# Six key blocks to a batch, and norms, reciprocals and layouts that keep channels on partitions

## The chip, the core and the metric

The kernel runs on one core of one Trainium2 chip. The metric is the device time of one execution in microseconds (us). Five engines work side by side, each on its own queue of instructions in program order: PE (TensorE, matrix products into PSUM), DVE (VectorE), ACT (ScalarE), POOL (GpSimd) and SP (SyncE, which issues DMAs here). They wait for each other by semaphores.

## What is computed

A block of depthwise convolution and attention over four images of 384 channels and 48 x 48 pixels (2304 tokens), in float32:

```python
x_flat = x.reshape(B, C, N).transpose(0, 2, 1)
local = lax.conv_general_dilated(x, conv_w, ..., feature_group_count=C)   # 7 x 7, one filter per channel
local = local * inv[None, :, None, None] + (bn_beta - bn_mean * inv)[None, :, None, None]
x_norm = _layernorm(x_flat, ln_gamma, ln_beta)
q, k, v = split(x_norm @ qkv_w.T + qkv_b)                # 8 heads of 48
q = q + heads(_layernorm(local_flat, ln_gamma, ln_beta))
attn = jax.nn.softmax(jnp.einsum('bhnd,bhmd->bhnm', q, k) * scale, axis=-1)
out = jnp.einsum('bhnm,bhmd->bhnd', attn, v)
out = x_flat + out @ proj_w.T + proj_b
```

## The kernel before

Channels lie on 128 partitions, in three chunks. A **tile** is one image's group of 384 tokens (8 pixel rows): 6 groups of 4 images make 24 tiles. For each tile the queries of the eight heads are held as four pairs (two heads of 48 rows, at partitions 0 and 64). For each pair, `attention` runs over the 18 blocks of 128 keys: two score products (L455) into a PSUM tile `s`, one exponential on ACT (L463, 128 x 768) into `pt`, and two products with the values (L431) that accumulate into `o`; a column of ones beside the values gives the sum of the exponentials. Blocks are taken two to a batch (`BATCH`): the scores of a batch are issued, then the value products of the batch before.

The rest is put beside that as generators in a deque, `behind`, of which a few steps are taken per batch: `q_part` (the 147 convolution taps of the next tile on DVE, L266 and L270, then the layer norms and the query projection L207), `kv_part` (keys and values of the next image, L207 and L229), `pair_output` and `group_output` (division and output projection L379). Norms want the tokens on partitions: `normalized` transposes each 128 x 128 block on PE (L153), takes mean and variance on DVE (L157, L158), the inverse root on POOL (L161), normalizes on DVE (L165), and `x_normalized` transposes back (L191). The convolution's norm is transposed back at L288, the attention output before its division at L343 (after copies out of PSUM on ACT and DVE, L439 and L440) and after it at L369.

A scheduler in the tile framework sets the final order of each engine's queue from the order in which the code is written and from its own estimate of when things are ready. The engines then keep that order on the chip.

A branch after the pass repeats the work with shifted exponents if a sum of exponentials was out of range (`inside`); in the profile shown here it is not taken.

Of the kernel before, what the change touches and what calls it, by code (L numbers as in the profile page):

```python
# [14 lines left out]
P = 128  # L15
NH = 8
# [4 lines left out]
BATCH = 2  # L21
RG = 8
SAFE = 1e15
AHEAD = 1
# [5 lines left out]

@with_exitstack
def attention_pass(
# [13 lines left out]
    shifted: bool,  # L48
    inside=None,
# [14 lines left out]
    HS = HA if shifted else HD  # L64
# [3 lines left out]
    kv = ctx.enter_context(tc.tile_pool(name="kv", bufs=NG + AHEAD))  # L68
    ps_s = ctx.enter_context(tc.tile_pool(name="ps_s", bufs=2, space=bass.MemoryType.PSUM))
    ps_o = ctx.enter_context(tc.tile_pool(name="ps_o", bufs=2, space=bass.MemoryType.PSUM))  # L70
    ps_m = ctx.enter_context(tc.tile_pool(name="ps_m", bufs=2, space=bass.MemoryType.PSUM))
# [263 lines left out]
    def pair_output(b, g, p, osb):  # L335

        if p == 0:
            outputs[b, g] = work.tile([P, NB, NH, HD], F32, tag="ao", name="ao", bufs=1)
        ao = outputs[b, g]
        tp = psum()  # L340
        ot = tp[:, :G].rearrange("p (t h d) -> p t h d", t=NB, h=2)
        for blk in range(NB):
            nc.tensor.transpose(  # L343
                tp[:, blk * P : blk * P + KP],
                osb[0:KP, blk * P : (blk + 1) * P],
                ident[0:KP, 0:KP],
            )
        rden = work.tile([P, NB, 2, 1], F32, tag="rden", name="rden")
        nc.vector.reciprocal(rden, ot[:, :, :, HD:HA])
        if inside is not None:  # L350

            flat = rden.rearrange("p t h o -> p (t h o)")
            for bound, op in ((SAFE, ALU.is_le), (1 / SAFE, ALU.is_ge)):
                nc.vector.scalar_tensor_tensor(inside, flat, bound, inside, op, ALU.mult)
# [57 lines left out]
    weighing = []  # L412
    divisions = deque()

    def weigh_last():
        if weighing:
            weighing.pop()()

    def attention(b, g, p, ahead, units):


        q = queries[b, g][p]
        o = ps_o.tile([P, 512], F32, tag="o", name="o")
        osb = work.tile([P, G], F32, tag="osb", name="osb")
        nc.gpsimd.memset(osb[32:64, :], 0.0)  # L425

        def weigh(batch):
            for kb, pt in batch:
                for j in range(2):
                    r = 64 * j  # L430
                    nc.tensor.matmul(  # L431
                        o[r : r + HA, :G],
                        lhsT=values[b, kb // NB][:, kb % NB, 2 * p + j, :],
                        rhs=pt[:, j, :],
                        start=kb == 0,
                        stop=kb == KB - 1,
                    )
            if batch[-1][0] == KB - 1:
                nc.scalar.copy(osb[0:HA, :], o[0:HA, :G])  # L439
                nc.vector.tensor_copy(osb[64 : 64 + HA, :], o[64 : 64 + HA, :G])  # L440
                divisions.append((b, g, p, osb))

        for k0 in range(0, KB, BATCH):
            while divisions:
                done = divisions.popleft()
                if done[2] == NP - 1:
                    behind.appendleft(group_output(*done[:2]))
                behind.appendleft(pair_output(*done))
            batch = []
            for kb in range(k0, k0 + BATCH):  # L450
                s = ps_s.tile([P, 2, 512], F32, tag="s", name="s")
                blk = kb % NB
                for j in range(2):
                    r = 64 * j
                    nc.tensor.matmul(  # L455
                        s[:, j, :G],
                        lhsT=keys[b, kb // NB][r : r + HS, p, blk * P : (blk + 1) * P],
                        rhs=q[r : r + HS, :],
                        start=True,
                        stop=True,  # L460
                    )
                pt = work.tile([P, 2, G], F32, tag="pt", name="pt", bufs=2 * BATCH)
                nc.scalar.activation(pt, s[:, :, :G], AF.Exp, scale=SCALE)  # L463
                batch.append((kb, pt))
            weigh_last()
            weighing.append(lambda batch=batch: weigh(batch))
            for _ in range(BATCH):
                if ahead is not None:
                    next(ahead, None)
            advance(BATCH * units)  # L470
        if ahead is not None:
            for _ in ahead:
                pass

# [4 lines left out]
    for b in range(B):  # L479
        if shifted:  # L480
            for _ in max_part(b, 0, 0):
                pass
        for g in range(NG):
            for p in range(NP):
                ahead = None
                if p == (NP - 1 if shifted else 0):
                    finish()
                if shifted and p < NP - 1:
                    ahead = max_part(b, g, p + 1)
                elif shifted and g < NG - 1:  # L490
                    ahead = max_part(b, g + 1, 0)
                if p == 0:
                    if g < NG - 1:
                        behind.append(q_part(b, g + 1))
                    elif b < B - 1:
                        for ga in range(AHEAD):
# [4 lines left out]
                attention(b, g, p, ahead, 5 if shifted else 3)  # L501
        weigh_last()
        while divisions:
            behind.append(pair_output(*divisions.popleft()))
        behind.append(group_output(b, NG - 1))
        if b < B - 1:
            for ga in range(AHEAD, NG):
                behind.append(kv_part(b + 1, ga))
        finish()


def conv_attention(tc: tile.TileContext, *args):
    nc = tc.nc
    with tc.tile_pool(name="keep", bufs=1) as keep:
        inside = keep.tile([P, 6], F32, tag="inside", name="inside")
        outside = keep.tile([P, 6], F32, tag="outside", name="outside")
        ones = keep.tile([P, 1], F32, tag="ones_col", name="ones_col")
        total = keep.tile([1, 1], F32, tag="total", name="total")
        flag = keep.tile([1, 1], mybir.dt.int32, tag="flag", name="flag")
        nc.vector.memset(inside, 1.0)  # L520
        nc.vector.memset(ones, 1.0)
        attention_pass(tc, *args, shifted=False, inside=inside)
        nc.vector.tensor_scalar(outside, inside, 0.5, None, ALU.is_lt)
        with tc.tile_pool(name="ps_f", bufs=1, space=bass.MemoryType.PSUM) as ps_f:
            count = ps_f.tile([1, 6], F32, tag="count", name="count")
            nc.tensor.matmul(count, lhsT=ones, rhs=outside, start=True, stop=True)
            nc.vector.tensor_reduce(total, count, AX.X, ALU.add)
        nc.vector.tensor_copy(flag, total)
        n_outside = nc.values_load(flag[0:1, 0:1])
        with tc.If(n_outside > 0):  # L530
            attention_pass(tc, *args, shifted=True)
# [51 lines left out]
```

## Time and profile before

| | us |
|---|---|
| median of 3 runs (lowest, highest) | 4068.94 (4068.04, 4070.35) |
| profiled execution | 4069.32 |
| its span | 4067.5 |
| PE busy in it | 3792.6 (93%) |
| DVE busy | 2347.7 (58%) |
| ACT busy | 1695.6 (42%) |
| mean granted TensorE clock | 0.947 of full |

A matmul of float32 operands shows as two records in the profile, so the 3456 calls of L455 are 6912 records. Matmul ends are modelled, so a busy PE is not a PE at its peak: start-to-start distances tell more than durations. A releaser in brackets names what ended an engine's idle time.

### The profile page before, as it was taken

How to read it: one execution, taken by the hardware profiler on the slowest of the kernel's cores; microseconds unless marked ns; L12 is line 12 of the kernel's file. 1: busy time of each engine (PE TensorE's matmuls, PEld its weight loads, DVE VectorE, ACT ScalarE, POOL GpSimd, SP SyncE). 2: the span in 40 equal slices, each digit the busy share in tenths (PEclk: the TensorE clock that was granted, in tenths of full speed). 3: DMA queues.
4: the chain of work that ended last, by engine and by line, in shares of the span. 5: the costliest groups of instructions: out<-in, count | busy, mean ns of one | idle time of the engine just before them, and what ended most of it. 6: DMA issues, size and time to landing. Idle time of an engine off the chain costs nothing.

```text
span 4067.5 us, 45598 instructions
## 1 busy us (share of the span) xinstructions
PE 3792.6 (93%) x17714; PEld 1655.5 (41%) x17714; DVE 2347.7 (58%) x4908; ACT 1695.6 (42%) x2449; POOL 189.5 (5%) x325
## 2 busy tenths in 40 slices
PE   5889999999999999999999998999999999999999
PEld 3434433344454343334445333433344433333443
DVE  7577647647553584674564548548548364764610
ACT  1244343453434434445433443443443344344444
POOL 1000000000000000000000000000000000000000
PEclk9889899999999999999999999999999999999999
DMA  2000000000000000000000000000000000000000
GB/s 61 1 1 7 5 3 6 3 39 6 7 0 1 7 6 1 7 6 36 7 6 1 1 7 7 1 7 6 36 7 6 1 1 7 7 3 5 7 7 7
DMA packets 20419, 33.97 MB, mean 8 GB/s; under 512 B 8416, under 2 KB 18656, under 8 KB 18656
## 3 DMA queue, kind: packets, MB, share of 16 engines
q1 hardware_dynamic: 12096, 28.32, 1.8%
q10 hardware_dynamic: 8096, 2.65, 0.3%
q8 instruction: 140, 2.29, 0.2%
q14 instruction: 87, 0.71, 0.1%
HBM read 16.80 MB, written 14.16 MB: 8 GB/s over the span
## 4 chain that ended last, share of the span: by engine, by line
PE 61%; DVE 34%; POOL 2%; issue 1%; ACT 1%; DMA 0%; ACTq 0%; POOLq 0%; DVEq 0%
DVE acc L270 27%; PE s L455 24%; PE o L431 20%; PE pm L207 7%; PE pm L379 3%; PE pm L229 2%; DVE st L157 2%; PE pm L191 2%; POOL rs L161 1%; DVE xt L165 1%; PE pm L153 1%; DVE q L293 1%; PE pm L343 1%; PE pm L369 1%; DVE osb L440 1%
## 5 line engine op out<-in xcount | busy, mean ns | idle before, releaser
L270 DVE SCALAR_TENSOR_TENSOR acc<-x,cw,acc 128x368 f32<-128x368 f32 (+10 forms) x3456 | 1872.1, 589 | 35.4
L463 ACT ACTIVATE pt<-s 128x768 f32<-128x768 f32 x1728 | 1316.1, 808 | 1307.2 <-PE s L455 1306.8
L455 PE MATMUL s<-q,k 48*128 48x384 f32 x6912 | 1551.1, 526 | 1.2 <-ACT pt L463 1.2
L431 PE MATMUL o<-pt,v 128*49 128x384 f32 x6912 | 1330.6, 505 | 0.0
L455 PEld LDWEIGHTS s<-q,k 48*128 48x128 f32 x6912 | 648.8, 190 | 697.3 <-ACT pt L463 364.7
L431 PEld LDWEIGHTS o<-pt,v 128*49 128x49 f32 x6912 | 381.8, 125 | 825.5 <-issue 823.3
L440 DVE COPY osb<-o 49x384 f32<-49x384 f32 x96 | 53.8, 560 | 759.5 <-ACT osb L439 757.8
L207 PE MATMUL pm<-xnT,w_qk 128*128 128x384 f32 x1152 | 424.8, 517 | 0.3 <-ACT q L214 0.3
L157 DVE BATCH_NORM_STATS2 st<-xt 128x6 f32<-128x384 f32 x216 | 113.4, 551 | 409.8 <-ACT xt L154 408.8
L207 PEld LDWEIGHTS pm<-xnT,w_qk 128*128 128x128 f32 x1152 | 219.7, 200 | 183.3 <-issue 24.8
L191 PE MATMUL pm<-ident,xt 128*128 128x128 f32 x432 | 103.4, 354 | 107.2 <-DVE xt L165 99.9
L194 ACT ACTIVATE xnT<-pm,ln_sb 128x384 f32<-128x384 f32 x144 | 92.4, 669 | 238.6 <-PE pm L191 238.6
L154 ACT COPY xt<-pm 128x384 f32<-128x384 f32 x216 | 98.2, 481 | 217.2 <-PE pm L153 183.1
L379 PE MATMUL pm<-aoT,w_o 128*128 128x384 f32 x432 | 182.1, 578 | 0.0
L343 PE MATMUL pm<-ident,osb 113*128 113x113 f32 x288 | 51.1, 288 | 105.9 <-DVE osb L440 105.9
L214 ACT ACTIVATE q<-pm,qkb 128x384 f32<-128x384 f32 x96 | 55.8, 581 | 224.7 <-PE pm L207 224.7
L229 PE MATMUL pm<-w_v,xnT 128*128 128x384 f32 x432 | 144.0, 487 | 5.4 <-DVE v L236 5.4
L191 PEld LDWEIGHTS pm<-ident,xt 128*128 128x128 f32 x432 | 60.5, 168 | 194.2 <-issue 75.7
L236 DVE TENSOR_TENSOR v<-pm,vb 128x384 f32<-128x384 f32 x72 | 39.9, 555 | 154.4 <-PE pm L229 154.3
L379 PEld LDWEIGHTS pm<-aoT,w_o 128*128 128x128 f32 x432 | 96.7, 234 | 75.4 <-issue 31.6
L425 POOL MEMSET osb<- 32x384 f32 x96 | 39.9, 416 | 1802.1 <-PE pm L343 1648.7
L214 ACT ACTIVATE k<-pm,qkb 128x384 f32<-128x384 f32 x96 | 55.8, 581 | 147.3 <-PE pm L207 147.3
(52 smaller groups left out, 1047.7 us busy)
## 6 DMA issues: line engine op xcount, KB each, us to landing
x<-in_x_dram SPq DMA_DIRECT2D x12, 1152.0 KB, 7.5
out_dram<-xr SPq DMA_DIRECT2D x72, 192.0 KB, 1.8
w_qk<-in_qkv_wT_dram ACTq DMA_DIRECT2D x6, 192.0 KB, 5.0
w_v<-in_qkv_wT_dram ACTq DMA_DIRECT2D x3, 192.0 KB, 5.6
w_o<-in_proj_wT_dram ACTq DMA_DIRECT2D x3, 192.0 KB, 3.7
vb<-in_v_b_dram ACTq DMA_DIRECT2D x1, 192.0 KB, 4.5
cw<-in_conv_w_dram ACTq DMA_DIRECT2D x1, 73.5 KB, 5.8
ln_p<-in_ln_pair_dram ACTq DMA_DIRECT2D x2, 1.5 KB, 4.5
```

The costliest lines, as they stand in the source:

```text
L154: nc.scalar.copy(xt[:, blk, :], tp[:, :C])
L157: nc.vector.bn_stats(st[:, blk, :], xt[:, blk, :])
L191: nc.tensor.transpose(tp[:, blk * P : (blk + 1) * P], kept["xn"][:, blk, c * P : (c + 1) * P], ident)
L207: nc.tensor.matmul(ps[:, :G], lhsT=w_qk[:, c, which, 2 * p : 2 * p + 2, :].rearrange("p h d -> p (h d)"), rhs=xnT[:, c, :], start=c == 0, ...
L214: nc.scalar.activation(dst, ps[:, :G], AF.Identity, bias=qkb[:, which, p : p + 1])
L229: nc.tensor.matmul(ps[:, :C], lhsT=xnT[:, c, blk * P : (blk + 1) * P], rhs=w_v[:, c, :], start=c == 0, stop=c == CC - 1,)
L270: nc.vector.scalar_tensor_tensor(dst, src, cw[:, c, t : t + 1], dst, ALU.mult, ALU.add)
L379: nc.tensor.matmul(ps[:, :G], lhsT=w_o[:, c, co * P : (co + 1) * P], rhs=aoT[:, c, :], start=c == 0, stop=c == CC - 1,)
L431: nc.tensor.matmul(o[r : r + HA, :G], lhsT=values[b, kb // NB][:, kb % NB, 2 * p + j, :], rhs=pt[:, j, :], start=kb == 0, stop=kb == KB - 1,)
L440: nc.vector.tensor_copy(osb[64 : 64 + HA, :], o[64 : 64 + HA, :G])
L455: nc.tensor.matmul(s[:, j, :G], lhsT=keys[b, kb // NB][r : r + HS, p, blk * P : (blk + 1) * P], rhs=q[r : r + HS, :], start=True, stop=True,)
L463: nc.scalar.activation(pt, s[:, :, :G], AF.Exp, scale=SCALE)
```

## The change

The pass that runs is written anew as `unshifted_pass`; the old function remains as `shifted_pass` behind the branch. What is different in the new one:

- **Layout.** Weights and activations are loaded so that rows 0 to 47 and 64 to 111 of the three chunks hold heads 0 to 5, and rows 48 to 63 and 112 to 127 hold a third each of heads 6 and 7 (`segments`). Queries and keys come from 3 instead of 4 projections; six small DMAs (`gather_tails`) collect the last two heads into one more tile, and six give them back after attention.
- **Norms.** Sums over chunks on DVE (`chunk_sum`), a matmul with a matrix of 1/384 that leaves the mean on every partition (`spread_mean`), subtraction on DVE and square on ACT (`centre`), the same again for the variance, the inverse root by Ln and Exp on ACT (`inverse_root`) with one Newton step on DVE. No PE transposes are left. Gain and offset go into the weights once.
- **Division.** The sums go to DRAM as one row per head (`den`), come back as 128 x 24, one reciprocal is taken, it goes to DRAM again (`rden`) and comes back spread over partitions (`rb`); one product divides the tile (`divide`, one per tile).
- **Batches.** Six key blocks to a batch, so three batches to a pair and 12 **slots** to a tile. PSUM: three score tiles of two banks (`ring`), one bank for the outputs (`sums`), one for all else (`bank`). `pt` has nine buffers.
- **Convolution.** From slabs of the image (`load_slab`), two accumulators `acc`, the taps spread over slots (`convolve`). Keys and values of the next image are made between images (`keys_values`), all six groups in a row; its x is normalized during the image before.

```diff
-BATCH = 2
+BATCH = 6
+NSLOT = 12
+X_SLOT, OUT_SLOT, LN_SLOT = 3, 5, 9
...
+    def chunk_sum(src):
+        s = work.tile([P, G], F32, tag="sum", name="sum")
+        nc.vector.tensor_add(s, src[:, 0, :], src[:, 1, :])
+        nc.vector.tensor_add(s, s, src[:, 2, :])
+        return s
...
+        nc.tensor.matmul(m[:, :G], lhsT=mean_w, rhs=s, start=True, stop=True)
...
+    def centre(src, m):
+        nc.vector.tensor_sub(src, src, over_chunks(m[:, :G]))
+        sq = work.tile([P, CC, G], F32, tag="sq", name="sq", bufs=1)
+        nc.scalar.activation(sq, src, AF.Square)
+        return sq
...
+        nc.scalar.activation(u, m[:, :G], AF.Ln, bias=eps)
+        nc.scalar.activation(y, u, AF.Exp, scale=-0.5)
+        nc.scalar.activation(u, y, AF.Square)
...
+    def newton(m, y, u):
+        nc.vector.scalar_tensor_tensor(u, m[:, :G], eps, u, ALU.add, ALU.mult)
+        nc.vector.scalar_tensor_tensor(u, u, -1.0, y, ALU.add, ALU.mult)
+        nc.vector.scalar_tensor_tensor(y, u, -0.5, y, ALU.mult, ALU.add)
...
+    def query_end(t, rs):
...
+        nc.vector.tensor_mul(acc, acc, over_chunks(rs))
+        for c in range(CC):
+            nc.vector.scalar_tensor_tensor(
+                q[:, c, :], acc[:, c, :], gain[:, c : c + 1], q[:, c, :], ALU.mult, ALU.add
+            )
+        gather_tails(q3, q)
...
+    def divide(t):
...
+        nc.sync.dma_start(out=rd, in_=den.rearrange(flat, f=few))
+        nc.vector.reciprocal(rd, rd)
+        nc.sync.dma_start(out=rden.rearrange(flat, f=few), in_=rd)
...
+    for t in range(NT):
+        b, g = divmod(t, NG)
+        if g == 0 and b:
+            weigh()
+            for gk in range(NG):
+                convolve(("kv", t, gk), 0)
+                keys_values(b, gk)
+                convolve(("kv", t, gk), 1)
...
+        for s in range(NSLOT):
+            point = ("slot", t, s)
+            scores(t, s)
+            convolve(point, 0)
...
+            if s < CC and following:
+                query_step(t + 1, s)
+            if s == X_SLOT and coming:
+                held["m"] = spread_mean(held.pop("s"))
+                held["sq"] = centre(xn[b + 1, g], held.pop("m"))
+            if s == X_SLOT + 1 and coming:
+                m = spread_mean(held.pop("s"))
+                held["root"] = m, *inverse_root(m)
+            if s in range(OUT_SLOT, OUT_SLOT + CC) and t:
+                output_step(t - 1, s - OUT_SLOT)
+            if s == LN_SLOT and following:
+                held["m"] = spread_mean(held.pop("s"))
+                held["sq"] = centre(accs[t + 1], held.pop("m"))
+            if s == LN_SLOT + 1 and following:
+                m = spread_mean(held.pop("s"))
+                held["root"] = m, *inverse_root(m)
+            if weighing[0][0] != t or s:
+                weigh()
+            convolve(point, 1)
...
+            if s == LN_SLOT + 1 and following:
+                query_end(t + 1, newton(*held.pop("root")))
```

What the scheduler makes of it shows in the queues. **PE in the middle of a pair**, before: a row is a run of products, `s` are scores, `o` the value products, `k_2` and `v_2` the key and value group 2.

```order
L455 MATMUL s<-q_1_2_1631,k_2_357 128x384 x2
L455 MATMUL s<-q_1_2_1631,k_3_441 128x384 x2
L431 MATMUL o<-pt,v_2_358 49x384 x4
L455 MATMUL s<-q_1_2_1631,k_3_441 128x384 x4
L431 MATMUL o<-pt,v_2_358 49x384 x2
L431 MATMUL o<-pt,v_3_442 49x384 x2
```

The same place now; `r` is a score tile, `m` the query projection of the next tile, and line 446 stands for 455, line 459 for 431.

```order
L446 MATMUL r<-q_844,k_2_474 128x384 x6
L446 MATMUL r<-q_844,k_3_557 128x384 x6
L268 MATMUL m<-xn_2_124,w_qk 128x384 x3
L459 MATMUL o<-pt,v_0_293 49x384 x6
L459 MATMUL o<-pt,v_1_393 49x384 x6
```

Four scores alternated with four value products; now twelve alternate with twelve, with one other step between at most.

**DVE at a result that PE waits for**, before: taps (L270, `acc`), and among them the copy of a finished pair's output (L440), without which PE cannot transpose it at L343.

```order
L266 TENSOR_SCALAR acc_934<-x0_83,cw_94,shift_134 128x384
L270 SCALAR_TENSOR_TENSOR acc_934<-x0_83,cw_94,acc_934 128x8x47
L270 SCALAR_TENSOR_TENSOR acc_934<-x0_83,cw_94,acc_934 128x8x45
L270 SCALAR_TENSOR_TENSOR acc_934<-x0_83,cw_94,acc_934 128x8x46
L440 COPY osb_920<-o_919 49x384
```

DVE now, in slot 3 of the second tile: the subtraction of the mean from the next image's x (L245), more taps (L203), and the sums of squares (L234, L235 of `sq`) that PE needs for its matmul in slot 4.

```order
L245 TENSOR_TENSOR xn1_1_1610<-xn1_1_1610,m_1820 128x1152
L203 SCALAR_TENSOR_TENSOR acc3_2196<-slab0_3_1401,cw_182,acc3_2196 128x384
L203 SCALAR_TENSOR_TENSOR acc3_2196<-slab0_3_1401,cw_182,acc3_2196 128x8x47
L203 SCALAR_TENSOR_TENSOR acc3_2196<-slab0_3_1401,cw_182,acc3_2196 128x8x46
L203 SCALAR_TENSOR_TENSOR acc3_2196<-slab0_3_1401,cw_182,acc3_2196 128x8x45 x2
L234 TENSOR_TENSOR sum_1850<-sq_1823 128x384
L234 TENSOR_TENSOR sum_2158<-acc2_1406 128x384
L235 TENSOR_TENSOR sum_1850<-sum_1850,sq_1823 128x384
```

Between the end of the previous norm (`query_end`) and the first row of this piece stand 109 taps, one reciprocal and the division; the sums stand behind 114 taps. All taps here are those of `acc3`, one tile ahead of the norm that they stand in front of.

## Rows read from the trace of the kernel before

**Rows 1.** Costliest groups: line, operation, count, busy us, mean ns, idle before.

```profile
L270 DVE SCALAR_TENSOR_TENSOR acc<-x,cw,acc 128x368 f32<-128x368 f32 (+10 forms) x3456 | 1872.1, 589 | 35.4
L463 ACT ACTIVATE pt<-s 128x768 f32<-128x768 f32 x1728 | 1316.1, 808 | 1307.2 <-PE s L455 1306.8
L455 PE MATMUL s<-q,k 48*128 48x384 f32 x6912 | 1551.1, 526 | 1.2 <-ACT pt L463 1.2
```

**Rows 2.** PE's waits: who for whom, us in total, times, longest.

```profile
PE pm L343 <- DVE osb L440: 105.9, 34, 8.1
```

**Rows 3.** Order of time, DVE, 193 to 240 us: start, length, what, count.

```profile
193.02 35.07 DVE L270 SCALAR_TENSOR_TENSOR acc<-x,cw,acc 128x360 f32<-128x360 f32 x68
...
230.05 0.56 DVE L440 COPY osb<-o 49x384 f32<-49x384 f32 x1
...
234.37 0.20 DVE L349 RECIPROCAL rden<-pm 128x6 f32<-128x6 f32 x1
```

**Rows 4.** Order of time, PE, 212 to 238 us, with idle time before and its releaser.

```profile
230.67 0.83 PE L343 MATMUL pm<-ident,osb 113*128 113x113 f32 x3 [8.13 <-DVE osb L440]
231.43 2.93 PE L455 MATMUL s<-q,k 48*128 48x384 f32 x8
...
236.91 1.56 PE L455 MATMUL s<-q,k 48*128 48x384 f32 x8
```

**Rows 5.** Stretches: us, busy of PE, PEld, DVE, ACT, POOL, PEclk, DMA, GB/s.

```profile
231.00:237.00 6.00, 6.00 (x21) 2.09 (x19) 5.75 (x14) 1.62 (x2) 0.41 (x1) 0.52 0.01 3
237.00:258.00 21.00, 21.00 (x116) 8.26 (x118) 19.83 (x34) 11.06 (x15) 0.00 (x0) 1.00 0.00 1
```

**Rows 6.** Order of time, PE, 500 to 515 us.

```profile
505.36 0.92 PE L455 MATMUL s<-q,k 48*128 48x384 f32 x4
506.21 1.50 PE L431 MATMUL o<-pt,v 128*49 128x384 f32 x8
507.64 2.20 PE L379 MATMUL pm<-aoT,w_o 128*128 128x384 f32 x6
509.77 1.56 PE L455 MATMUL s<-q,k 48*128 48x384 f32 x8
511.26 1.50 PE L431 MATMUL o<-pt,v 128*49 128x384 f32 x8
512.69 1.56 PE L455 MATMUL s<-q,k 48*128 48x384 f32 x8
```

**Rows 7.** Order of time, all engines, exponentials at 510 us.

```profile
510.79 1.51 ACT L463 ACTIVATE pt<-s 128x768 f32<-128x768 f32 x2 [3.60 <-PE s L455]
```

**Rows 8.** Order of time, PE, key and value projections at 1145 us.

```profile
1144.79 7.91 PE L207 MATMUL pm<-xnT,w_qk 128*128 128x384 f32 x24
1152.54 5.97 PE L229 MATMUL pm<-w_v,xnT 128*128 128x384 f32 x18
```

**Rows 9.** Groups by form, the small operations that price new ones.

```profile
L165 DVE TENSOR_SCALAR xt<-xt,mv,rs 128x384 f32<-128x384 f32 x144 | 61.6, 483 | 55.4 <-POOL rs L161 55.4
...
L439 ACT COPY osb<-o 49x384 f32<-49x384 f32 x96 | 45.4, 473 | 60.1 <-PE o L431 56.3 <-issue 3.8
L386 DVE SCALAR_TENSOR_TENSOR xr<-pm,pb,xr 128x384 f32<-128x384 f32 x72 | 44.3, 615 | 43.7 <-PE pm L379 43.4
```

**Rows 10.** Order of time, the first taps, and the first score products.

```profile
15.95 8.69 DVE L270 SCALAR_TENSOR_TENSOR acc<-x,cw,acc 128x225 f32<-128x225 f32 x18
...
185.49 0.91 PE L455 MATMUL s<-q,k 48*128 48x384 f32 x2
```

**Rows 11.** DMA issues: what, count, KB each, median us from issue to landing.

```profile
out_dram<-xr SPq DMA_DIRECT2D x72, 192.0 KB, 1.8
...
cw<-in_conv_w_dram ACTq DMA_DIRECT2D x1, 73.5 KB, 5.8
```

**Rows 12.** Order of time, the last 15 us.

```profile
4054.09 7.13 PE L379 MATMUL pm<-aoT,w_o 128*128 128x384 f32 x18
...
4061.25 0.62 DVE L386 SCALAR_TENSOR_TENSOR xr<-pm,pb,xr 128x384 f32<-128x384 f32 x1 [1.32 <-PE pm L379]
```

More of the change, by code (lines that the diff above doesn't have):

```diff
@@ new lines, in conv_attention @@
+def conv_attention(tc: tile.TileContext, *args):
+    nc = tc.nc
+    few = NH * RG * 48 // P
+    with tc.tile_pool(name="keep", bufs=1) as keep:
+        inside = keep.tile([P, few], F32, tag="inside", name="inside")
+        outside = keep.tile([P, few], F32, tag="outside", name="outside")
+        ones = keep.tile([P, 1], F32, tag="ones_col", name="ones_col")
+        total = keep.tile([1, 1], F32, tag="total", name="total")
+        flag = keep.tile([1, 1], mybir.dt.int32, tag="flag", name="flag")
+        nc.vector.memset(inside, 1.0)
+        nc.vector.memset(ones, 1.0)
+        unshifted_pass(tc, *args, inside)
+        nc.vector.tensor_scalar(outside, inside, 0.5, None, ALU.is_lt)
+        with tc.tile_pool(name="ps_f", bufs=1, space=bass.MemoryType.PSUM) as ps_f:
+            count = ps_f.tile([1, few], F32, tag="count", name="count")
+            nc.tensor.matmul(count, lhsT=ones, rhs=outside, start=True, stop=True)
+            nc.vector.tensor_reduce(total, count, AX.X, ALU.add)
+        nc.vector.tensor_copy(flag, total)
+        n_outside = nc.values_load(flag[0:1, 0:1])
+        with tc.If(n_outside > 0):
+            shifted_pass(tc, *args)
@@ L50, in attention_pass, with shifted_pass @@
+@with_exitstack
+def shifted_pass(
+    ctx: ExitStack,
+    tc: tile.TileContext,
+    x: bass.AP,
+    conv_w: bass.AP,
+    bn: bass.AP,
+    ln: bass.AP,
+    ln_pair: bass.AP,
+    qk_b: bass.AP,
+    v_b: bass.AP,
+    qkv_wT: bass.AP,
+    proj_wT: bass.AP,
+    proj_b: bass.AP,
+    out: bass.AP,
 ):
@@ L425, in attention @@
         nc.gpsimd.memset(osb[32:64, :], 0.0)
[L427 to L470, printed above, removed]
@@ new lines, in weigh @@
+        def weigh(kb, pt):
+            for j in range(2):
+                r = 64 * j
+                nc.tensor.matmul(
+                    o[r : r + HA, :G],
+                    lhsT=values[b, kb // NB][:, kb % NB, 2 * p + j, :],
+                    rhs=pt[:, j, :],
+                    start=kb == 0,
+                    stop=kb == KB - 1,
+                )
+        last = None
+        for kb in range(KB):
+            s = ps_s.tile([P, 2, 512], F32, tag="s", name="s")
+            blk = kb % NB
+            for j in range(2):
+                r = 64 * j
+                nc.tensor.matmul(
+                    s[:, j, :G],
+                    lhsT=keys[b, kb // NB][r : r + HA, p, blk * P : (blk + 1) * P],
+                    rhs=q[r : r + HA, :],
+                    start=True,
+                    stop=True,
+                )
+            pt = work.tile([P, 2, G], F32, tag="pt", name="pt", bufs=3)
+            nc.scalar.activation(pt, s[:, :, :G], AF.Exp, scale=SCALE)
+            if ahead is not None:
+                next(ahead, None)
+            if last is not None:
+                weigh(*last)
+            last = (kb, pt)
+            advance(units)
@@ L471, in attention @@
+        weigh(*last)
         if ahead is not None:
@@ L500, in attention_pass @@
                     load_x(b + 1)
[L501 to L505, printed above, removed]
+                attention(b, g, p, ahead, 5)
         if b < B - 1:
-            for ga in range(AHEAD, NG):
+            for ga in range(1, NG):
                 behind.append(kv_part(b + 1, ga))
         finish()
[L512 to L531, printed above, removed]
 def kernel(**inputs):
```

420 lines of the change are left out of this document (394 added, 26 removed).

## The prediction, made before the changed kernel ran

> **What bounds the kernel now.** I began with the groups and the waits. PE is never long without work of its own (93% busy), scores and exponentials pair off as 6912 records and 1728 exponentials, and ACT waits for PE, not PE for ACT [rows 1]. What PE waits for in the list of waits is DVE, above all the copy of a finished pair (L440) [rows 2]. The order of time shows why: at 193 us DVE starts 68 taps that end at 228.1, and the copy that PE wants stands behind them and three more [rows 3]. PE ends its products, waits 8.1 us, and then needs 5.48 us (231.43 to 236.91) for scores and value products of two blocks [rows 4]. The same work takes 2.92 us from 509.77 to 512.69 [rows 6]. [...] So a wait of 8 us cost another 2.6 us. The bound is therefore PE's own work, plus the places where DVE's queue, full of taps, holds back a result that PE needs.
>
> **PE's own work.** One block's scores take 0.85 us (505.36 to 506.21), two blocks' 1.49 (509.77 to 511.26): 0.64 a block and 0.21 for the change of kind [rows 6]. Two blocks' value products take 1.43, by the same slope 0.14 + 2 x 0.64 [rows 6]. Six to a batch then cost 4.05 + 4.00 = 8.05 us a slot, against 3 x 2.92 = 8.76 for three batches before; 288 slots save 204 us. Three projection calls take 2.13 (507.64 to 509.77) [rows 6]; 24 records in a row take 7.75, 0.323 each [rows 8], so a mean (one call, two records) costs 2.13 - 4 x 0.323 = 0.84. A tile has 12 slots, three query steps, three output steps and four means: 96.6 + 12.8 + 3.4 = 112.8 us, and 24 tiles 2707. Off that: 10.7 in the first tile (no output before it, two query steps done earlier), 10.1 for means of a next image that the last six tiles don't have, 8.1 for the last tile's query and norm: 28.9. That leaves **2678**. Keys and values are 18 calls a group, 36 x 0.323 + 0.3 = 11.9 us; 18 groups between images make **214**; those of the first image fall in the start. All transposes go, four query and four key projections become three, and nothing of that stands elsewhere.
>
> **Copies of a pair** (ACT, two of 0.47 [rows 9]) delay the next exponentials. The second exponential of a batch ends 0.755 us after the first (two in 1.51 [rows 7]), three to half a slot of 4 us, so ACT has about 0.8 us of room there; the first score needs 1.0 us anyway before an exponential can start (509.77 to 510.79 [rows 6, 7]). I take 0.2 us of delay for each of 96 pairs, **20** (ends 0 and 0.95 x 96 = 91).
>
> **The start.** Taps begin at 15.95 before [rows 10]; the constants now pass through DRAM, one landing more (1.8 to 5.8 [rows 11]), so about 18. The queue of DVE holds 268 taps before the first queries are complete: 147 of the first tile at 0.49 (18 short ones take 8.69 [rows 10]) and 121 of the second at 0.516 (35.07 / 68 [rows 3]), 134 us. Beside them stand seven norms of 6.1 (two sums 1.8, subtraction 1.35, Newton 1.65, product 1.3; by rows 9, an operation of 384 takes 0.48 to 0.62, and one of 1152 about three times the streaming part), 18 value additions of 0.5, and 3. That is 207, and I add 13 for five norms that wait for PE and ACT by 2 to 3 us each. **220** (ends 200 and 245), where scores began at 185 before [rows 10].
>
> **The end.** After the last value product: copies 1.2, four DMA hops one after the other, reciprocal 0.2 [rows 3], product 1.3, projection 7.2 and one addition 0.6 [rows 12], and 5.6 from there to the end (4061.87 to 4067.5 [rows 12]). A hop costs 1.8 to 5.8 [rows 11]; I take 3, since these are small but go to DRAM and back. **28** (24 to 39).
>
> [...] No row here shows a DRAM round trip.
>
> **What DVE's queue does to PE.** This is the term that decides. Measured from the end of `query_end` (T = 0), DVE has in a middle tile 58 taps, the reciprocal and its tests, 22 taps, the division, 29 taps, the subtraction of x's mean, 5 taps and three sums before PE's matmul of slot 4 has its input. By 0.516 that is 58.8 + 0.5 + 1.3 + 1.35 + 1.3 = 63.3. PE meanwhile: slot 10's mean ends 5 us into slot 10; Ln, Exp and Square stand around three exponentials and end at 9; Newton, product and three additions end at 13.6. T = 0 is therefore 4.7 us into slot 11, and the next slot 0 begins at T = 3.3. Slots 0 to 2 with queries take 30.5, slot 3 8.9, and the scores of slot 4 4.05: PE stands at the matmul at T = 46.8. It waits 16.5 us, and loses about 2.6 more to the clock, as at 231 us [rows 4, 5]. The wait that would follow in slot 5 (0.9 us, the bank is held until Newton has read it) lies inside those 2.6. That makes 19.1 us for each of 15 tiles (five in each of the first three images; in tiles with edge taps there are six to ten more taps, each cheaper). In three tiles of the last image 147 taps stand before the addition that frees the bank in slot 5: done at T = 75.8 + 2.4 = 78.2, wanted at 64.1, 14.1 + 2.6 = 16.7 each. In the first tile 87 taps give 47.5 against 35.5: 14.6. No tile that follows a key phase waits, since its taps are done by then. Sum 287 + 50 + 15 = **352**. The reciprocal itself must be back by T = 30: the pair's end at 13.5, copies 1.2, two hops of at most 5.8 give 26.3. `rb` must be there at T = 41.7: two hops more, 30.2 + 11.6 = 41.8. So that covers the round trip even at the longest of these two landings; beyond it, each us of a hop pair moves the whole queue, 18 x 1 us.
>
> [...]
>
> **Sum.** 2678 + 214 + 20 + 220 + 28 + 352 = 3512 us of span. The profiled execution took 4069.32 at a span of 4067.5, so 1.8 goes on top: **3514 us**. The median of the runs, 4068.94, is 0.4 below that execution, which changes nothing here.
>
> **Rivals.**
>
> *DVE does not hold PE back.* If everything else holds, 3514 - 352 = 3162. For that a tap must cost under (46.8 - 4.5) / 114 = 0.371 us. Against it: 0.516 in the longest run, and the very same wait in the trace of before [rows 2 to 4].
>
> *Taps cost more in the new queue.* The mean busy time of a tap over the whole trace is 589 ns [rows 1]; with 0.073 more than my 0.516, 15 x 8.3 + 3 x 10.7 + 6 + 20 = 183 more: 3697. For it: slabs are new operands, and more foreign instructions stand between. Against it: the long runs of taps are longer than before.
>
> *Slower than before, by the clock.* After each of 19 waits PE has some 62 us of work until the next norm. The trace shows half speed for 6 us after a wait [rows 5]. If the clock stayed at the lower level until the next norm, each wait would cost 62 us: 3514 + 19 x 62 = 4690. It decides from (4069 - 3514) / 19 = 29 us of PE's full-speed work done at half speed after each wait. Against it: the return to 1.00 after 237 [rows 5], with the same kind of work following.
>
> *The change does not do what it says.* The queues show no transposes left and twelve products in a row, so only the branch could bring old work back. It hangs on the same test of sums of exponentials as before, which did not take it.
>
> **How the numbers follow.** About what a measurement of this kernel can tell from no change is 0.2%. I give 63% to the forecast (3400 to 3640: 5 us either way on each of 19 waits, start and copies between their ends), 15% to dearer taps (3640 to 3760), 14% to a smaller or absent wait (7% at 3290 to 3400, 7% below), 4% to more than 3760 and yet faster, 4% to slower. The range 3290 to 3740 leaves out the lowest case and the top of the others, 17 in 100. Faster 0.95, within 0.2% 0.01, slower 0.04.
>
> **What would show it.** Right, if the profile of the changed kernel has scores and value products of a slot in 8.0 to 8.1 us from start to start; if PE's longest waits are for sums of squares on DVE (L235), 15 of 14 to 19 us, with runs of taps ahead of them; if the granted clock drops to half after each; if the first value products come at 220; if ACT has no share in PE's waits beyond some tens of us. Wrong, if taps run at another rate than 0.516, if DVE waits at the reciprocal or at the division for a DMA, if ACT's squares, which stand between exponentials, make scores wait for a PSUM tile, or if the clock takes longer to come back.

## The result, and the profile after

The changed kernel takes 3587.79 us (median of four, 3586.07 to 3591.69) against 4068.49 before: ratio 0.8819, interval 0.8804 to 0.8834. The prediction said 3514, range 3290 to 3740. The profiled execution took 3587.64 at a span of 3585.8; all that follows is read from it.

PE's own work has shrunk much more than the time has. The first part of the page (busy us, share of the span, instructions) reads for the changed kernel:

```profile
PE 3128.2 (87%) x15788; PEld 1400.6 (39%) x15788; DVE 2296.8 (64%) x4287; ACT 1579.6 (44%) x2275; POOL 8.5 (0%) x39
```

PE was busy 93% of the span before and is 87% now, and part of that at half clock (granted 0.50 from 393 to 397 us, for one). The list of waits (who for whom, us in total, times, longest) tells what it waits for:

```profile
PE r L446 <- ACT pt L450: 274.8, 17, 17.8
PE m L268 <- DVE xr L424: 50.5, 5, 18.4
...
ACT sq L247 <- DVE xn L245: 294.6, 22, 17.9
```

These answer [rows 2]. The wait for DVE that was 105.9 us in 34 pieces has become one long wait a tile, and most of it wears another name: PE waits at its scores for an exponential of ACT, and ACT waits at the square of the norm (L247) for DVE's subtraction (L245). The order of time around such a wait, DVE, ACT and PE (start, length, what, count; idle time and its releaser in brackets):

```profile
382.81 6.36 DVE L203 SCALAR_TENSOR_TENSOR acc<-slab,cw,acc 128x360 f32<-128x360 f32 x10
389.09 1.35 DVE L245 TENSOR_TENSOR xn<-xn,m 128x1152 f32<-128x1152 f32 x1
390.47 1.16 ACT L247 ACTIVATE sq<-xn 128x1152 f32<-128x1152 f32 x1 [17.48 <-DVE xn L245]
392.52 2.21 ACT L450 ACTIVATE pt<-r 128x768 f32<-128x768 f32 x3
393.38 4.21 PE L446 MATMUL r<-q,k 48*128 48x384 f32 x12 [17.36 <-ACT pt L450]
```

DVE goes through its taps and reaches the subtraction at 389.09. ACT's square has stood in its queue for 17.48 us, with the exponentials behind it; PE has filled its score tiles and waits for those. The clock follows, as in [rows 5]. The stretches (us; busy PE, PEld, DVE, ACT, POOL; PEclk, DMA, GB/s):

```profile
360.00:376.00 16.00, 16.00 (x89) 6.55 (x87) 16.00 (x33) 7.23 (x10) 0.00 (x0) 1.00 0.39 76
377.00:393.00 16.00, 0.00 (x0) 0.00 (x0) 15.50 (x28) 2.48 (x4) 0.00 (x0) 0.57 0.00 1
393.00:403.00 10.00, 9.62 (x38) 3.89 (x38) 9.57 (x18) 5.37 (x9) 0.00 (x0) 0.67 0.00 0
403.00:420.00 17.00, 17.00 (x90) 7.90 (x88) 15.53 (x27) 6.64 (x9) 0.00 (x0) 1.00 0.04 13
```

Between 377 and 393 PE has nothing at all and DVE 15.5 of 16 us. After that the granted clock is 0.67 in the mean for 10 us, then full again.

Where nothing holds it, PE runs through its slots like this (order of time, PE, in the last tile):

```profile
3517.43 4.21 PE L446 MATMUL r<-q,k 48*128 48x384 f32 x24
3521.56 4.08 PE L459 MATMUL o<-pt,v 128*49 128x384 f32 x24
3525.57 4.21 PE L446 MATMUL r<-qt,kt 48*128 48x384 f32 x24
```

A slot lasts 8.14 us from start to start. Three batches of two took 8.76 before [rows 6].

### The profile page after: what moved, and what is told of

It reads as the page before. It is cut to its first block, busy times and chain, and to the rows that moved or that the text cites. A ratio compares the mean times of both kernels' runs of the same rounds, so it can differ in the third digit from the quotient of the medians.

```text
span 3585.8 us, 41771 instructions
## 1 busy us (share of the span) xinstructions
PE 3128.2 (87%) x15788; PEld 1400.6 (39%) x15788; DVE 2296.8 (64%) x4287; ACT 1579.6 (44%) x2275; POOL 8.5 (0%) x39
## 4 chain that ended last, share of the span: by engine, by line
PE 49%; DVE 45%; ACT 3%; issue 2%; DMA 1%; SPq 0%; DVEq 0%; ACTq 0%
DVE acc L203 38%; PE r L446 21%; PE o L459 19%; PE m L268 5%; PE m L241 2%; ACT pt L450 2%; PE r L268 1%; DVE q L357 1%; DVE v L306 1%; DVE acc L355 1%; DVE acc L199 1%; DVE xn L245 1%; DVE ao L544 1%; DVE u L260 0%; ACT ao L376 0%
## 5 line engine op out<-in xcount | busy, mean ns | idle before, releaser
L203 DVE SCALAR_TENSOR_TENSOR acc<-slab,cw,acc 128x368 f32<-128x368 f32 (+8 forms) x3456 | 1835.6, 587 | 32.4
L450 ACT ACTIVATE pt<-r 128x768 f32<-128x768 f32 x1728 | 1279.1, 811 | 960.1 <-PE o L459 593.8
L446 PE MATMUL r<-q,k 48*128 48x384 f32 x5184 | 956.5, 515 | 288.4 <-ACT pt L450 273.2
L446 PEld LDWEIGHTS r<-q,k 48*128 48x128 f32 x5184 | 455.2, 192 | 779.9 <-ACT pt L450 504.2
L446 PE MATMUL r<-qt,kt 48*128 48x384 f32 x1728 | 304.5, 498 | 1.6 <-ACT pt L450 1.6
L245 DVE TENSOR_TENSOR acc<-acc,m 128x1152 f32<-128x1152 f32 x24 | 32.5, 1354 | 364.4 <-PE m L241 364.4
L268 PE MATMUL m<-ao,w_o 128*128 128x384 f32 x432 | 166.6, 524 | 57.5 <-DVE xr L424 50.5
L446 PEld LDWEIGHTS r<-qt,kt 48*128 48x128 f32 x1728 | 147.0, 185 | 158.9 <-ACT pt L450 79.1
L268 PE MATMUL r<-xn,w_qk 128*128 128x384 f32 x432 | 155.1, 516 | 25.3 <-issue 21.6
L268 PE MATMUL m<-xn,w_qk 128*128 128x384 f32 x432 | 161.5, 511 | 4.5 <-DVE u L260 2.4
L247 ACT ACTIVATE sq<-xn 128x1152 f32<-128x1152 f32 x24 | 27.9, 1164 | 294.6 <-DVE xn L245 294.6
L268 PE MATMUL r<-w_v,xn 128*128 128x384 f32 x432 | 143.2, 486 | 0.0
L268 PEld LDWEIGHTS m<-ao,w_o 128*128 128x128 f32 x432 | 79.3, 197 | 138.2 <-DVE xr L424 55.8
```

Of the source, the lines that this page charges most:

```text
L203: nc.vector.scalar_tensor_tensor(dst, src, weight, dst, ALU.mult, ALU.add)
L245: nc.vector.tensor_sub(src, src, over_chunks(m[:, :G]))
L268: nc.tensor.matmul(dst, lhsT=weights(c), rhs=src(c), start=c == 0, stop=c == CC - 1)
L446: nc.tensor.matmul(r[:, j, :G], lhsT=kk[:, blk * P : (blk + 1) * P], rhs=qq, start=True, stop=True)
L450: nc.scalar.activation(pt, r[:, :, :G], AF.Exp, scale=SCALE)
```

## The experiments

A *tile* in this table is the time from the first query projection made in one tile to the first one made in the next, *middle* the mean over twelve tiles inside the first three images, *last* that of three tiles of the last image. *Start* is the first score product. All from profiled executions; the times are medians.

| kernel | us | start | middle tile | last tiles |
|---|---|---|---|---|
| changed | 3587.8 | 218.8 | 135.4 | 131.4 |
| x norm in slots 7, 8 | 3581.9 | 219.5 | 132.9 | 131.1 |
| that and outputs in 8 to 10 | 3405.2 | 218.1 | 124.4 | 114.0 |
| square on DVE | 3577.9 | 218.4 | 134.3 | 131.3 |
| taps in written order | 3273.6 | 219.8 | 120.9 | 112.6 |
| taps left out | 3164.2 | 205.0 | 114.2 | 112.5 |
| written order, batches of 3 | 3331.5 | 217.0 | 122.6 | 115.7 |
| written order, chunks alternating | 3226.7 | 264.0 | 114.2 | 112.5 |
| that, start rewritten | 3143.3 | 183.3 | 114.2 | 112.6 |
| x norm and outputs late, alternating | 3309.5 | 217.5 | 118.9 | 114.0 |
| alternating alone | 3566.6 | 219.6 | 135.4 | 125.4 |
| more hops | 3591.6 | 219.6 | 135.2 | 131.4 |

**Is it DVE's queue, and is it its order?** The theory: the queue, in which the scheduler put 109 taps ahead of the subtraction, holds PE. The rivals: the square on ACT is the cause by itself, or DVE has too much to do.

*Taps bound to the written order* (each tap is queued behind all DVE work written ahead of it; line numbers behind it grow by 3):

```diff
-                    nc.vector.tensor_scalar(
+                    ins = nc.vector.tensor_scalar(
...
-                    nc.vector.scalar_tensor_tensor(dst, src, weight, dst, ALU.mult, ALU.add)
+                    ins = nc.vector.scalar_tensor_tensor(
+                        dst, src, weight, dst, ALU.mult, ALU.add
+                    )
+                tc.keep_in_program_order(ins)
```

> Each convolution tap is bound to stand on DVE's queue behind all DVE work written ahead of it, so that the 12 taps of a slot stay in their slot. Theory (DVE's queue, full of hoisted taps, holds PE): the 19 long waits of PE (322 us) and what the lower clock costs after each (about 3.4 us for 16 of them, 2.8 for three, 62 in all) go, and the start loses the 115 taps of the second tile that stood ahead of the first queries, 59 us: 3588 - 322 - 62 - 59 = 3145, range 3120 to 3190. Rival 1 (the square on ACT, which stands among the exponentials, is what holds PE, whatever DVE does): only the start gains, about 3530. Rival 2 (written order makes DVE wait for PE and fall behind in other places): over 3250, with new waits of PE at sums (L237, L238) or at the query sum.

Measured 3273.63. The waits of PE, and the first score (which was at 218.84):

```profile
PE r L449 <- ACT pt L453: 45.9, 16, 4.6
PE m L244 <- DVE sum L238: 31.5, 5, 14.3
```

```profile
219.75 8.37 PE L449 MATMUL r<-q,k 48*128 48x384 f32 x48
```

The same work in another order on one engine gains 314 us, and the first rival falls. But the range was missed by 84, for two reasons. The start did not move, though 112 taps were taken out of the way of the first queries (156 instead of 268 stand ahead of them). And waits of 3.3 to 4.6 remain in twelve tiles, 6.7 us a tile with the clock, and one of 14.3 in the first tile: there the second rival is right in part. In written order DVE now stands at the reciprocal until its DMA has landed, some 5 us in a tile, and then comes late to the norm of x. That this stand is the cause was not tested by itself; the kernel with alternating chunks below stands there even longer (236.6 us in all against 164.1) and has no wait of PE left in its middle tiles; the taps behind it run at 0.518 us each instead of 0.637. The wait of DVE (47.0 of it at the end, where DVE has nothing else):

```profile
DVE rd L397 <- DMA rd<-den: 164.1, 24, 47.0
```

*The norm of x later*, without anything bound, and *both x and the outputs later*:

```diff
-X_SLOT, OUT_SLOT, LN_SLOT = 3, 5, 9
+X_SLOT, OUT_SLOT, LN_SLOT = 7, 5, 9
```

```diff
-X_SLOT, OUT_SLOT, LN_SLOT = 3, 5, 9
+X_SLOT, OUT_SLOT, LN_SLOT = 7, 8, 9
```

> One constant: the norm of the next image's x moves from slots 3 and 4 to slots 7 and 8; the output steps stay in slots 5 to 7. In DVE's queue all 147 taps now stand ahead of the residual additions of the output steps. Theory (whatever DVE result PE wants first in the middle of a tile waits for the taps): 15 waits of 17.5 us at scores become 15 of about 18.4 at the output step in slot 6, as in the last image, the first tile loses its wait of 10: about 3590, range 3560 to 3620. Rival (the wait belongs to the norm of x, or to its square on ACT): 16 waits of 20 with their clock go, about 3255.

> Two constants: the norm of the next image's x in slots 7 and 8, the output steps in slots 8 to 10. DVE's queue still has all 147 taps in one run after the query is done. Theory: the taps end at about 78 us after the query is done, the norm of x is wanted at 45.5 + 4 x 8.15 = 78, so that no long wait is left: 3588 - 384 = 3204, range 3190 to 3260 (the start stays at 219). Rival (DVE has too much work, not the wrong order): over 3400, waits of PE in slots 8 to 11 instead.

The first gave 3581.89: moving the step that waits gains next to nothing, because the next one in line waits in its place. Its waits of PE:

```profile
PE m L268 <- DVE xr L424: 289.8, 20, 18.4
```

The second gave 3405.18. It gains, so what matters is how PE's demand lies to the end of the run of taps; but it lies 200 above what was expected, and just above the bound of the rival (too much work for DVE, over 3400). Its order of time, DVE and PE, shows the reason, which is new:

```profile
524.43 31.20 DVE L203 SCALAR_TENSOR_TENSOR acc<-slab,cw,acc 128x360 f32<-128x360 f32 x49
555.54 1.35 DVE L245 TENSOR_TENSOR xn<-xn,m 128x1152 f32<-128x1152 f32 x1
...
558.83 4.21 PE L446 MATMUL r<-q,k 48*128 48x384 f32 x12 [8.21 <-ACT pt L450]
```

These 49 taps take 0.637 us each, not 0.515. They are the third chunk's. The queue alternates the taps of the first two chunks, so that a tap never continues the sum of the one just before it; the third chunk is left alone.

*The square on DVE* instead of ACT:

```diff
-    def centre(src, m):
+    def centre(src, m, on_dve=False):
...
-        nc.scalar.activation(sq, src, AF.Square)
+        if on_dve:
+            nc.vector.tensor_mul(sq, src, src)
+        else:
+            nc.scalar.activation(sq, src, AF.Square)
...
-                held["sq"] = centre(xn[b + 1, g], held.pop("m"))
+                held["sq"] = centre(xn[b + 1, g], held.pop("m"), True)
```

> The square in the norm of the next image's x is taken by DVE (a product) instead of ACT; 109 taps still stand ahead of the subtraction. Theory (DVE's queue is the cause, ACT only passes the wait on to the exponentials): PE waits at the averaging matmul (L241) instead, 15 times 15 to 17 us, as the prediction had it: about 3565, range 3540 to 3600. Rival (the blocked exponentials are the cause): the waits go, 3588 - 330 = about 3260.

Measured 3577.92. PE's waits:

```profile
PE m L241 <- DVE sum L235: 263.0, 18, 16.5
```

ACT only passes the wait on. With it out of the way PE waits at the averaging matmul, where the prediction had it, for nearly as long.

**What is PE's own work, and what sets the start?** The convolution left out but for its middle taps:

```diff
-                if r0 >= r1:
+                if r0 >= r1 or tap != taps[0]:
                     continue
```

> The changed kernel without its convolution, but for the middle tap of each chunk: 144 of 147 taps of a tile are left out, so that DVE has next to nothing in its queue. Theory (taps ahead of wanted results cost 384 us, and the start hangs on the chain of norms and projections, not on the taps, since it stayed at 219 with 115 taps fewer ahead): 3588 - 384 = 3204 and at most 15 less in the start, 3180 to 3210. The prediction's own account of the start (the sum of what DVE has to do): 268 taps less, 134 us, so 3070 to 3100.

Measured 3164.18, 16 below the range: no long wait is left, a middle tile takes 114.2, and scores begin at 205. So 262 taps (6 instead of 268 stand ahead of the first queries) weighed 14 us in the start, not 134. What sets it reads, in the order of time, as a chain, one group of tokens after the other (21.0 us apart from the second on): the norm (mean, square, mean, root), then the projections.

**What does a batch cost?** Three blocks to a batch in the kernel with taps in written order:

```diff
-BATCH = 6
-NSLOT = 12
-X_SLOT, OUT_SLOT, LN_SLOT = 3, 5, 9
+BATCH = 3
+NSLOT = 24
+X_SLOT, OUT_SLOT, LN_SLOT = 6, 10, 18
```

> The kernel with taps in written order, and three key blocks to a batch instead of six (24 slots to a tile, the steps in slots of twice the number). Prediction's term (a change between scores and value products costs 0.21 + 0.14 = 0.35 us): 288 more pairs of changes, 101 us more than six to a batch, 3274 + 101 = 3375, range 3350 to 3395. Rival (the change is hidden, and six to a batch gains only by what ACT or DVE do beside it): 3274, or less, since what is due in a slot comes in smaller pieces.

Measured 3331.49, 58 more, and 19 below the range. The order of time of PE:

```profile
3022.38 2.14 PE L462 MATMUL o<-pt,v 128*49 128x384 f32 x12
3024.46 2.21 PE L449 MATMUL r<-q,k 48*128 48x384 f32 x12
3026.59 2.14 PE L462 MATMUL o<-pt,v 128*49 128x384 f32 x12
```

A batch of three takes 4.21 us, so two of them 8.42 against 8.14: 0.28 for one more pair of changes, not 0.35. In the last tiles, where nothing waits, that is what is seen: 3.2 us for 12 more batches. In the middle tiles only 1.7 of it arrive; there PE waits for DVE anyway (81.0 us in 36 waits over the whole kernel), which probably hides the rest. The rival (no cost) falls; the size was off by a fifth for one change, and by two fifths in the total (58 instead of 101).

**Is a tap slower behind a tap of its own chunk?** The taps written with the chunks inside, in the kernel with taps in written order:

```diff
-        for c in range(CC):
-            img = slab[:, c, : (end - first) * W].rearrange("p (h w) -> p h w", w=W)
-            a = acc[:, c, :].rearrange("p (h w) -> p h w", w=W)
-            for tap in taps:
...
+        for tap in taps:
...
+            for c in range(CC):
+                img = slab[:, c, : (end - first) * W].rearrange("p (h w) -> p h w", w=W)
+                a = acc[:, c, :].rearrange("p (h w) -> p h w", w=W)
```

> As the kernel with taps in written order, but with the taps written tap by tap over the three chunks instead of chunk by chunk, so that a tap never follows another of the same chunk. Theory (a tap that continues the sum of the one just before it takes 0.637 us from start to start, one that follows a tap of another chunk 0.515): runs of taps at 0.515 throughout, 147 x 0.12 = 18 us less for DVE in a tile, and the 12 waits of 3.3 to 4.6 at the norm of x with their clock (2 to 3 us each) and the wait of 14 in the first tile go or shrink: 3274 - 46 - 30 - 8 = 3190, range 3180 to 3225. Rival (the slower taps come from the place of the rows or from what runs beside them): runs at 0.637 still, and 3274.

Measured 3226.68. The order of time of DVE in a middle tile, and one row of PE in the start:

```profile
502.64 16.07 DVE L203 SCALAR_TENSOR_TENSOR acc<-slab,cw,acc 128x368 f32<-128x368 f32 x31
```

```profile
166.84 1.65 PE L244 MATMUL m<-sum,mean_w 128*128 128x384 f32 x2 [13.37 <-DVE u L263]
```

Taps of all three chunks now take 0.518, and the middle tiles are at 114.2, as without any convolution: the taps are hidden completely. That the total missed the range by 2 is the start's doing: the queue now has 24 taps ahead of the Newton step (L263) of four groups, 13 us each on the chain that sets the start, and scores begin 44 us later.

*The start rewritten* on top of that: the norm of the next group stands between the parts of `keys_values`, the first tile's queries are projected a group later, the reciprocal is asked for in slot 1, and SP loads the output weights. This is the version that beats both kernels.

```diff
-            nc.scalar.dma_start(out=dst[p0 : p0 + piece.shape[0]], in_=piece)
+            queue = nc.scalar if dst is w_v else nc.sync
+            queue.dma_start(out=dst[p0 : p0 + piece.shape[0]], in_=piece)
...
+            if between:
+                between[u0 // 2]()
...
-        if g == 0:
...
+        if g == 1:
...
-        keys_values(0, g)
+        keys_values(0, g, steps)
...
-            if s == 0 and t:
+            if s == 1 and t:
                 held["rb"] = divide(t - 1)
```

> The kernel before it in this list, with three more edits: the norm of a group in the start is written between the parts of the keys and values of the group before; the reciprocal is asked for one slot later; the output weights and the projection's offset are loaded by SP instead of ACT. Theory (the start is a chain of norm and projections, 21.5 us a group, of which 14.3 is PE's own work): 5 x 5 us less, some 10 less for half speed after the waits and up to 8 for ACT's DMA issues, so 30 to 45 less than the kernel before it: about 3150. Rival (taps set the start): no change there.

Measured 3143.28, ratio to the kernel before 0.7723 (0.7710 to 0.7736). It is 83 less than the kernel before it in the list, not 30 to 45, because that one had made the start longer first; against the changed kernel's start of 218.8 it is 36 less. All 147 taps of the first tile stand ahead of the first queries, as in the kernel before it, so the rival (taps set the start) falls. But the 36 do not come as the theory had it, 5 us a group. The first key projections stand at 59.6 instead of 68.7, the second group's follow 20.5 us later instead of 36.8, and the others 20.5 apart instead of 22.0. What sets those 20.5 us, with the norm out of the way, stays open. The first score, and the page's busy times:

```profile
183.25 8.37 PE L452 MATMUL r<-q,k 48*128 48x384 f32 x48
```

```profile
PE 3050.9 (97%) x15788; PEld 1371.3 (44%) x15788; DVE 2235.3 (71%) x4287; ACT 1573.1 (50%) x2275; POOL 8.5 (0%) x39
```

**Does the slow third chunk explain the 200 us?** Late steps with alternating taps, and alternating taps as the only edit; neither binds anything.

> The norm of the next image's x in slots 7 and 8 and the output steps in 8 to 10, as in the second of those two moves, and the taps written tap by tap over the three chunks; nothing is bound, so all 147 taps still stand in one run ahead of the norm of x. Theory (what kept that kernel at 3405 was the third chunk's 49 taps at 0.637 us): the run ends 6 us earlier, the waits of 8.2 shrink to some 1 to 2 us, the first tile's wait of 27 by about 12: 3405 - 10 x 6 - 12 - some of the clock after short waits = 3290, range 3240 to 3330. Rival (DVE is simply short of time when the work is late): within 20 of 3405.

> The changed kernel with nothing but the taps written tap by tap over the three chunks. In DVE's queue 112 taps instead of 109 stand ahead of the subtraction of the mean of x. Theory: the waits at the norm of x stay (109 taps were at 0.515 already), only the three waits in the last image lose 6 us each, since all 147 taps stand ahead there: about 3588 - 18 + 15 x 1.5 = 3590, range 3560 to 3605. Rival (the slow taps are a large part of the loss): under 3540.

Measured 3309.52 and 3566.62. In the first, the last 68 of the 147 taps now end in time:

```profile
504.15 35.07 DVE L203 SCALAR_TENSOR_TENSOR acc<-slab,cw,acc 128x368 f32<-128x368 f32 x68
539.13 1.35 DVE L247 TENSOR_TENSOR xn<-xn,m 128x1152 f32<-128x1152 f32 x1
```

The 8.2 us waits fell to 2.3 or less, and half of the excess went. What keeps this kernel 83 above the one with taps in written order and alternating chunks (whose start is 47 longer at that) is in the first tile, where 174 taps stand ahead (138.2 against 116.3), in the three key phases (14.6 us each), and in the middle tiles (118.9 against 114.2): six of the twelve have a short wait of 1.9 to 2.3 us, after which 12 records of scores take 2.32 to 4.21 us, against 2.21 where nothing holds them. The same taps at the same rate leave no such wait in written order, so this too is order and not the amount of work. In the second, the middle tiles are unchanged and the last ones lose 6.0: there all 147 taps stand ahead, elsewhere almost only fast ones.

**Does the trip through DRAM cost anything?** Two more copies on it:

```diff
-        nc.sync.dma_start(out=rd, in_=den.rearrange(flat, f=few))
+        nc.sync.dma_start(out=den2, in_=den)
+        nc.sync.dma_start(out=rd, in_=den2.rearrange(flat, f=few))
...
-        nc.sync.dma_start(out=rden.rearrange(flat, f=few), in_=rd)
+        nc.sync.dma_start(out=rden2.rearrange(flat, f=few), in_=rd)
+        nc.sync.dma_start(out=rden, in_=rden2)
```

> The changed kernel with two more copies in DRAM on the way of the reciprocal: one of the sums before they are read, one of the reciprocals before they are spread. Theory (in a tile the trip is hidden: the reciprocal stands behind 58 taps, the division behind 22 more, and neither waited): nothing in the tiles, 4 to 6 us at the end, where the hops stand one behind the other: 3593, range 3588 to 3600. Rival (the trip is on DVE's path, where it moves all that follows): 23 x 4 us, 3680.

Measured 3591.57, 3.8 more, with middle tiles unchanged. The end, from the last pair's copy (ACT) to the division (DVE), in the changed kernel and in this one:

```profile
3554.09 0.97 ACT L376 COPY aot<-o 49x384 f32<-49x384 f32 x2 [4.82 <-PE o L459]
...
3555.40 3.67 SPq L381 DMA_DIRECT2D ao<-aot  x6
3559.17 0.53 SPq L393 DMA_DIRECT2D rd<-den  x1
...
3567.89 1.36 DVE L553 TENSOR_TENSOR ao<-ao,rb 128x1152 f32<-128x1152 f32 x1 [5.08 <-DMA rb<-rden]
3569.30 4.21 PE L268 MATMUL m<-ao,w_o 128*128 128x384 f32 x6 [6.94 <-DVE ao L553]
...
3579.38 0.62 DVE L424 SCALAR_TENSOR_TENSOR xr<-m,pb,xr 128x384 f32<-128x384 f32 x1 [2.29 <-PE m L268]
```

```profile
3554.66 0.97 ACT L376 COPY aot<-o 49x384 f32<-49x384 f32 x2 [4.82 <-PE o L463]
...
3572.57 1.36 DVE L557 TENSOR_TENSOR ao<-ao,rb 128x1152 f32<-128x1152 f32 x1 [7.18 <-DMA rb<-rden]
```

13.80 us have become 17.91, 2.05 for a hop, and the tiles hide all of it.

## Why the prediction was right, and where its steps were off

The forecast fell 74 us short, on the span (3512 against 3585.8). Most of that, 61 us, is one term, the waits; another 14 is PE's own work and the end.

**PE's own work.** Forecast 2678 + 214 + 20 + 28 = 2940; without taps, from the first score to the end, 3159.3 - 205.0 = 2954. A tile was put at 112.8 and 0.8 for copies; it takes 114.2. The saving per slot was read a little large: per block 0.64 from the difference of two rows, where six in a row show 8.14 a slot instead of 8.05 (288 slots, 26 us). The pair copies, on the other side, cost 0.1 us each, not 0.2 (scores of 3507.06 to 3511.29 beside a copy, 4.23, and 4.13 without).

**The waits.** Forecast 352; the changed kernel needs 3585.8 - 218.8 = 3367 from the first score to the end, 413 more than without taps. By places:

- *Middle tiles:* 15 times 19.1 was forecast, 21.2 measured (135.4 - 114.2). The count was exact and the step that failed was the place. The prediction followed DVE's queue to the sum that PE's next matmul needs, and passed over ACT, whose in-order queue has the square between exponentials; it named this at the end as a way to be wrong. PE stops three score tiles earlier, half a slot, and waits 17.4 to 17.8 where 16.5 was forecast. The square on DVE restores the forecast place, with waits of 15.8 to 16.6.
- *The clock* after each: 3.6 where [rows 4, 5] had given 2.6. PE resumes with half its score tiles still to fill: 4.14 us for 12 records at half speed (granted 0.50 from 393 to 397) instead of 2.07, then a mean and value products.
- *Last image:* 14.1 + 2.6 forecast, 21.2 in two of the three tiles. The 0.516 us of [rows 3] holds for two alternating chunks, and the last 48 taps ran alone:

```profile
2936.01 28.87 DVE L203 SCALAR_TENSOR_TENSOR acc<-slab,cw,acc 128x360 f32<-128x360 f32 x56
...
2987.52 30.67 DVE L203 SCALAR_TENSOR_TENSOR acc<-slab,cw,acc 128x360 f32<-128x360 f32 x48
...
3018.77 4.21 PE L268 MATMUL m<-ao,w_o 128*128 128x384 f32 x6 [18.37 <-DVE xr L424]
```

  0.516 and 0.639 each. The trace of before has the slower rate too, just behind [rows 3] (order of time, DVE, 226 to 246 us), 0.637 each:

```profile
235.46 10.83 DVE L270 SCALAR_TENSOR_TENSOR acc<-x,cw,acc 128x360 f32<-128x360 f32 x17
```

  The prediction took its price of a full tap from the longest run alone. The rival of dearer taps was thus right for one chunk in three. The mean of busy times on which it rested says little, since records of neighbouring taps overlap (0.59 us busy, 0.516 from start to start).
- *First tile:* 14.6 forecast, 17.0 measured (127.2 against 110.2 without taps).
- *Key phases:* none forecast, 7.6 for each of three: PE's first scores need the score tiles that the values of the last group still hold until DVE (L306), behind taps, has taken them (two waits in each phase, 15.2 us in all six).

**The start.** Forecast 220, measured 218.8, and yet the account of it was wrong. It summed DVE's work; but with 112 taps less it stayed, and with 262 less it lost 14. The chain of norm and projections (22.0 us a group, 21.0 without taps) is the likelier account: rewriting it took 36 us off with the taps still there, though which link sets the distance of the groups is open. That DVE's sum was as long was luck. An agreement in one term is no proof of its mechanism.

**The end.** 28 forecast, 31.8 measured (3553.97 to 3585.8). The sum of the hops came out, 13.8 less the copy, 12.8, where 12.2 was forecast with the reciprocal; their price did not. An added hop costs 2.05, not 3, and the difference is a term that the forecast lacked: SP issues the six DMAs that give back the last heads (L381, 3.67 us) ahead of the read of the sums (L393). That the two errors cancel is luck. The three projections were too cheap, 10.7 instead of 7.8: the first runs at half clock (granted 0.50 from 3569 to 3573; 4.21 us instead of 2.20), and with one PSUM bank each of the others waits 0.71 for the addition before it.

**The other rivals.** DVE does not hold PE back: wrong by the trace, and 3164 without taps is its price of 3162 only because two errors cancel (14 us more for PE's own work and the end, 15 less in the start). The clock staying low: wrong, 1.00 within 10 us. The change not doing what it says: no branch was taken.

## What to carry to other kernels

When work on a spare engine is spread evenly in the source, look at what the scheduler made of it: here it packed 109 to 147 filler instructions ahead of results that PE needs, and PE waited, up to 18 us each time. Moving only the step that waits passes the wait to the next step (6 us gained), and moving both gains 183; binding the filler to its written place removes most of it (314), and writing the filler so that neighbours do not depend on each other took another 47 off here, although the start became 44 longer. And follow a wait through every in-order queue it crosses: the engine that is blamed (ACT here) may only hold the place in line.

## What the runs showed of the hardware

A tap that continues the sum of the tap just before it starts 0.637 us after it; one that follows a tap of another chunk 0.515 to 0.518, although each is busy for some 0.59. So independent neighbours overlap and dependent ones do not: in the last image of the changed kernel DVE is busy all through the 28.70 us of 56 alternating taps (2936.10 to 2964.80), and for 28.83 of the 30.50 us of the 48 taps that ran alone (2987.60 to 3018.10), 0.60 each. The difference, 0.12 us, is 18 us a tile here if all taps depend on their neighbours.

In the kernel with taps in written order a short wait of PE costs nearly as much clock as a long one does in the changed kernel, 3.0 us against 3.6. A wait of 3.25 us is followed there by half clock (0.50 from 505 to 508; stretches as above):

```profile
505.00:508.00 3.00, 3.00 (x12) 1.24 (x8) 2.89 (x6) 0.43 (x1) 0.00 (x0) 0.50 0.02 5
508.00:514.00 6.00, 6.00 (x30) 2.17 (x30) 5.68 (x11) 3.62 (x6) 0.00 (x0) 0.85 0.00 0
514.00:530.00 16.00, 16.00 (x84) 7.53 (x82) 10.60 (x17) 6.65 (x9) 0.00 (x0) 1.00 0.04 13
```

Its middle tile is 6.7 us longer than without taps, of which 3.7 is the wait (mean of twelve) and the rest, 3.0, the clock; in the changed kernel 3.6 us of clock follow waits of 17.4 to 17.8.
